# Prologue of a fused attention and FFN layer: FFN weight casts moved behind block 1's v, block 2's projections by seven products, last split of h behind a down product

## The chip, the cores and the metric

The kernel runs on one core of one Trainium2 chip, in one launch. The metric is device time in microseconds (us) from the first to the last instruction of that core; of several runs the median is told. Engines are named as in the profile: PE (TensorE, matrix products), PEld (its weight loads), DVE (VectorE), ACT (ScalarE), POOL (GpSimd), SP (SyncE, which only issues transfers here).

## The reference

There are 8192 tokens (4 x 2048) of 256 features. Everything is float32, and the FFN's weights arrive as int32.

```python
def _L0_attn_ref(x, W_q, W_k, W_v, W_g, W_o, log_decay):
    Q = x @ W_q.T; K = x @ W_k.T; V = x @ W_v.T
    mask = jnp.where(diff >= 0, decay ** diff, 0)          # within chunks of 32 tokens
    S = jnp.einsum('bncd,bnkd->bnck', Qc, Kc) * mask
    O = jnp.einsum('bnck,bnkd->bncd', S, Vc).reshape(B, T, D)
    gate = jax.nn.sigmoid(x @ W_g.T)
    return gate * O @ W_o.T + x

def _L0_ffn_ref(x, w_gate, w_up, w_down):                  # 256 -> 768 -> 256, int32 / 127
    h = jax.nn.silu(x @ wg.T) * (x @ wu.T)
    return h @ wd.T

x = _layernorm(x + _L0_attn_ref(x, ...))
x = _layernorm(x + _L0_ffn_ref(x, ...))
```

The queries and keys appear only in their product, so the kernel forms M = W_q.T @ W_k once and uses y = x @ M in place of both.

## The kernel before

**Tiling.** The tokens go in 16 blocks of 512 (`NB`, `TB`). A block passes these steps, each a function: `attn_gate` (sg, L460), `attn_y` (yT, L476), `attn_v` (v, L495), `attn_scores` (sT, L515), `attn_values` (goT, L536), `attn_out` (h: the product pa, L562, residual and layer norm), then h is turned so that features lie on partitions, the FFN's gate and up products in six chunks (`ffn_up`, fg and fu, L657), and the down product with the second layer norm (`ffn_down` fdn, L562, and `finish`).

**Three ways to do a projection or a turn.** For blocks 0 to 2, gate, y and v are plain products (eight quarter products each, with a 2 x 2 split of both operands). From block 3 on `split_gate`, `split_y`, `split_v` do them by seven quarter products (`seven`, L364 and L380): the operands' sums are made by POOL (`weight_sums` once for each weight, `token_sums` once for each block); four products fill four PSUM banks, three of them are copied out by ACT (L407), one sum is made by DVE (L409) and one by POOL (L411); then `others()` adds three more products onto the banks, and ACT, DVE (twice) and POOL write the four quarters. Block 0's and the last block's h are turned by PE (`transpose_h`, tile pt, with the high part hT_hi by ACT at L602 and the low part hT_lo by DVE at L603). All other blocks' h are turned by DVE and 16 small transfers (`move_h`, sq and hT, L617 and L623) and then split (`split_h`: hT_hi by ACT at L640, hT_lo by POOL at L641).

**High and low parts.** The FFN's products are done with a high and a low part of their operands. `integers` (L253) makes both parts of each weight by ACT casts from the int32 tiles, six casts for each of the three weights. Between the FFN's products, ACT takes s (L665), DVE forms u (L667, L669), ACT casts u_hi (L676) and POOL makes u_lo (L677).

**What orders the work.** A scheduler places the instructions of each engine; casts, splits and a few others are held in the order in which they are written. [...] PSUM has eight banks (`bank`), and each new one waits until the last reader of the bank it takes over is done. Two tokens-by-features buffers (`xin`, two of each kind) carry x, so block 2's xT can be loaded once block 0's scores are done.

**Stages.** A prologue does attention for blocks 0 and 1 and the projections of block 2. Then a loop (L746) takes for b = 0 to 13 the FFN of block b, the rest of block b+2's attention, and the projections of block b+3. An epilogue (from L790) does the FFN of blocks 14 and 15. In the prologue PE's order is: gate and v of block 0, M, gate of block 1, y of block 0, v of block 1, scores of 0, y of 1, values of 0, scores of 1, pa of 0, values of 1, then **y and v of block 2 (plain), pa of 1, gate of block 2 (plain), the turn pt of block 0**, and the first FFN product. ACT's order there is: v of 1, a table load, rstd of block 0 (L305), **12 casts of fg and fu, v of block 2, rstd of block 1, six casts of fd, a table load, gate of block 2 (L467), hT_hi of block 0**.

In the loop, `split_h` of block b+1 is written ahead of the last `ffn_up` chunk (L769). That holds for b = 13 too, where block 14's h is split. On ACT its two casts stand ahead of the last u_hi, on POOL its two subtractions stand ahead of the last u_lo:

```python
        ffn_up(b, hT, uT, range(4, 5))
        y_rest()
        hTs[b + 1] = split_h(b + 1, moving)
        ffn_up(b, hT, uT, range(5, KH))
```

Of the kernel before, what the change touches and what calls it, by code (L numbers as in the profile page):

```python
# [63 lines left out]
H_UP = 2.0**23  # L64
# [6 lines left out]
def kernel(  # L71
# [18 lines left out]
    KD = D // P  # L90
    KH = H // P
    NB = NT // TB

    const = ctx.enter_context(tc.tile_pool(name="const", bufs=1))
    setup = ctx.enter_context(tc.tile_pool(name="setup", bufs=2))
# [43 lines left out]
    wv = load_w(nc.scalar, w_vT, "wv")  # L139
    wq = load_w(nc.sync, w_q, "wq")  # L140
    wk = load_w(nc.scalar, w_k, "wk")
    if NB > 1:
        xTs[1] = load_xT(1)
    wo = load_w(nc.scalar, w_oT, "wo")
    xns[0] = load_xn(0)
    if NB > 1:
        xns[1] = load_xn(1)


    def pieces_of(t, i):  # L150
# [303 lines left out]
    def attn_gate(b):  # L454
        xt = xTs[b]
        sg = work.tile([P, KD, TB], F32, tag="sg", name=f"sg_{b}")
        for dc in range(KD):
            pg = bank(f"pg_{b}_{dc}")
            for ec in range(KD):
                nc.tensor.matmul(  # L460
                    pg,
                    lhsT=wg[:, ec, dc * P : (dc + 1) * P],
                    rhs=xt[:, ec, :],
                    start=(ec == 0),
                    stop=(ec == KD - 1),
                )
            nc.scalar.activation(sg[:, dc, :], pg, AF.Sigmoid)  # L467
        return sg

    def attn_y(b):  # L470
        xt = xTs[b]
        yT = work.tile([P, KD, TB], F32, tag="yT", name=f"yT_{b}")
        for fc in range(KD):
            py = bank(f"py_{b}_{fc}")
            for ec in range(KD):
                nc.tensor.matmul(  # L476
                    py,
                    lhsT=m_sb[:, ec, fc * P : (fc + 1) * P],
                    rhs=xt[:, ec, :],
                    start=(ec == 0),  # L480
                    stop=(ec == KD - 1),
                )
            nc.vector.tensor_copy(yT[:, fc, :], py)
        return yT

    def attn_v(b):
        xt = xTs[b]
        v = work.tile([P, NG, D], F32, tag="v", name=f"v_{b}")
        per = TB // D
        for h in range(NG // per):  # L490
            pv = bank(f"pv_{b}_{h}")
            for j in range(per):
                g = h * per + j
                for ec in range(KD):
# [201 lines left out]
    def finish(b, r, start=None):  # L696
        layer_norm(r, r, f"f{b}", on_r=H_UP)
        store(b, r, start)


    hs, hTs = {}, {}
    ys = {}
    first, second = 0, min(1, NB - 1)
    sg, v = attn_gate(first), attn_v(first)
    make_m()
    if second:
        sg_second = attn_gate(second)
    ys[first] = attn_y(first)
    if second:
        v_second = attn_v(second)  # L710
    sT = attn_scores(first, ys.pop(first))
    if second:
        ys[second] = attn_y(second)
    goT = attn_values(first, sT, v, sg)
    if second:
        sT_second = attn_scores(second, ys.pop(second))
    hs[first] = attn_out(first, goT, 1 if NB == 1 else H_UP)
    fg = integers(ffn_gT, ffn_int[0], "fg")
    fu = integers(ffn_uT, ffn_int[1], "fu")
    if second:  # L720
        goT = attn_values(second, sT_second, v_second, sg_second)
    x_sums = {}
    ahead = {}
    if NB > 2:
        xTs[2] = load_xT(2)
        ahead[2] = attn_y(2), attn_v(2)
    if second:
        hs[second] = attn_out(second, goT, 1 if NB == 2 else H_UP)
    fd = integers(ffn_dT, ffn_int[2], "fd")
    if NB > 2:  # L730
        ahead[2] += (attn_gate(2),)
    if NB > 3:
        for w, name in ((m_sb, "m"), (wg, "g"), (wv, "v")):
            w_sums[name] = weight_sums(w, name)
        xTs[3] = load_xT(3)
        x_sums[3] = token_sums(xTs[3], "x_3")
    hTs[first] = transpose_h(first, hs[first], 1 if NB == 1 else H_UP)


    half = range(KH // 2), range(KH // 2, KH)  # L740
    looked = 0

    def nothing():
        pass

    for b in range(NB - 2):  # L746
        n = b + 2
        m = n + 1 if n + 1 < NB else None
        xns[n] = load_xn(n)
        hT = hTs.pop(b)  # L750
        uT = [], []
        yT, v, sg = ahead.pop(n)
        ffn_up(b, hT, uT, range(0, 2))
        sT = attn_scores(n, yT)
        if m is not None and m + 1 < NB:
            xTs[m + 1] = load_xT(m + 1)
        moving = move_h(b + 1, hs[b + 1])
        ffn_up(b, hT, uT, range(2, 3))
        v_rest = y_rest = g_rest = nothing
        if m is not None:  # L760
            v_next, v_rest = split_v(m, x_sums[m])
        ffn_up(b, hT, uT, range(3, 4))
        v_rest()
        goT = attn_values(n, sT, v, sg)
        if m is not None:
            y_next, y_rest = split_y(m, x_sums[m])
        ffn_up(b, hT, uT, range(4, 5))
        y_rest()
        hTs[b + 1] = split_h(b + 1, moving)  # L769
        ffn_up(b, hT, uT, range(5, KH))  # L770
        if m is not None:
            sg_next, g_rest = split_gate(m, x_sums.pop(m))
        hs[n] = attn_out(n, goT, 1 if n == NB - 1 else H_UP)
        g_rest()
        if m is not None:
            ahead[m] = y_next, v_next, sg_next
            if m + 1 < NB:
                x_sums[m + 1] = token_sums(xTs[m + 1], f"x_{m + 1}")
        finish(b, ffn_down(b, uT, hs.pop(b)))
        if looked < top.shape[1]:  # L780
            look_up(looked)
            looked += 1
# [8 lines left out]
    per = NG // 2  # L791
    cols = [slice(i * per * P, (i + 1) * per * P) for i in range(2)]
    uT_last = [], []
    early = range(0)
    if NB > 1:
        uT = [], []
        ffn_up(last - 1, hTs[last - 1], uT, half[0])
        hTs[last] = transpose_h(last, hs[last], 1)
        ffn_up(last - 1, hTs[last - 1], uT, half[1])
        early = half[0]  # L800
        ffn_up(last, hTs[last], uT_last, early, cols[0])
        r_before = ffn_down(last - 1, uT, hs[last - 1])
        mv_before = moments(r_before, f"f{last - 1}")
    ffn_up(last, hTs[last], uT_last, range(len(early), KH), cols[0])
    ffn_up(last, hTs[last], uT_last, range(KH), cols[1])
    n_wide = count_wide()
# [28 lines left out]
            )  # L835
            in_turn(scaled)

    if NB > 1:
        std_before = root(mv_before, f"f{last - 1}", H_UP, order=in_turn)
    r = work.tile([P, NG, D], F32, tag="r2", name=f"r2_{last}")  # L840

    def store_group(g):
# [12 lines left out]
    for g in range(NG):  # L855
        pb = bank(f"fdn_{last}_{g}")[:, :D]
        terms = back_terms(g, uT_last, map(chunked, fd))
        for i, (part, w) in enumerate(terms):
            nc.tensor.matmul(
                pb,  # L860
                lhsT=part[:, g * P : (g + 1) * P],
                rhs=w,
                start=(i == 0),
                stop=(i == len(terms) - 1),
            )
        in_turn(
            nc.vector.scalar_tensor_tensor(
                r[:, g, :], pb, SCALE**3 / U_UP, hs[last][:, g, :], ALU.mult, ALU.add
            )
        )  # L870
        mv = moments(r, f"f{last}_{g}", [g], order=in_turn)
        if g == 0 and NB > 1:
            normalize(r_before, mv_before, std_before, f"f{last - 1}", H_UP)
            store(last - 1, r_before)
        std = root(mv, f"f{last}_{g}", groups=[g], order=in_turn)
        waiting.append((g, mv, std))
        if 0 < g < NG - 1:
            normalize_first()
        if g == NG - 2:
            normalize_first()  # L880
# [119 lines left out]
```

## Time and profile before

| what | value |
|---|---|
| time, median of 3 runs | 545.64 us (544.54 to 545.95) |
| span of the profiled execution | 545.3 us |
| prologue, up to the first FFN product | 56.89 us |
| one pass of the loop (91.58 to 123.60) | 32.02 us |
| ACT_TABLE_LOAD (L305 group) | 1283 ns each |
| HBM traffic | 53 GB/s over the span |

The profile's busy times are shares of the whole span, and the 14 passes of the loop weigh most in them. The change touches the prologue, the first pass and the last pass, so those stretches have to be read by themselves: the list of waits, the chain of work that ended last, and the stretches cut at the first FFN product and at the last down product of the loop. A row of the timeline or of the chain has the start, the length in us, the engine, the tile and the line; times are from the span's start. In the table by stretch, each engine has its busy time and in brackets how many instructions; after them come the granted clock of PE as a share of full speed, the share of the DMA engines, and GB/s.

### The profile page before, as it was taken

How to read it: one execution, taken by the hardware profiler on the slowest of the kernel's cores; microseconds unless marked ns; L12 is line 12 of the kernel's file. 1: busy time of each engine (PE TensorE's matmuls, PEld its weight loads, DVE VectorE, ACT ScalarE, POOL GpSimd, SP SyncE). 2: the span in 40 equal slices, each digit the busy share in tenths (PEclk: the TensorE clock that was granted, in tenths of full speed). 3: DMA queues.
4: the chain of work that ended last, by engine and by line, in shares of the span. 5: the costliest groups of instructions: out<-in, count | busy, mean ns of one | idle time of the engine just before them, and what ended most of it. 6: DMA issues, size and time to landing. Idle time of an engine off the chain costs nothing.

```text
span 545.3 us, 9852 instructions
## 1 busy us (share of the span) xinstructions
PE 527.8 (97%) x3462; PEld 419.8 (77%) x3462; DVE 387.7 (71%) x1019; ACT 306.9 (56%) x551; POOL 261.1 (48%) x295
## 2 busy tenths in 40 slices
PE   8998899999999999999999999999999999998992
PEld 5676588887878888787888878788887878876792
DVE  4266457769686776968777596867859686796873
ACT  2216455666466565646646574664657566464744
POOL 5120164563637456372645737265572726333552
PEclk9999799999999999999999999999999999999998
DMA  7531301413123141311314131141413112020102
GB/s 256 169 116 40 77 2 40 117 39 98 21 54 102 40 112 44 97 22 49 106 40 111 45 95 24 47 109 40 108 48 88 31 44 73 2 73 5 40 2 81
DMA packets 43126, 36.87 MB, mean 68 GB/s; under 512 B 4673, under 2 KB 38977, under 8 KB 43073
## 3 DMA queue, kind: packets, MB, share of 16 engines
q1 hardware_dynamic: 41952, 35.15, 22.7%
q10 hardware_dynamic: 1088, 1.05, 0.6%
q8 instruction: 29, 0.48, 0.4%
q14 instruction: 25, 0.20, 0.1%
q0 software_dynamic: 32, 0.00, 0.0%
HBM read 20.45 MB, written 8.39 MB: 53 GB/s over the span
## 4 chain that ended last, share of the span: by engine, by line
PE 90%; DVE 3%; ACT 2%; SPq 1%; POOL 1%; issue 1%; DMA 0%; DVEq 0%; ACTq 0%
PE fg L657 16%; PE fu L657 15%; PE fdn L562 14%; PE pa L562 10%; PE p_v L380 7%; PE p_y L364 7%; PE p_g L364 7%; PE po L536 5%; PE ps L515 3%; PE py L476 2%; PE pv L495 2%; PE pg L460 1%; SPq L623 1%; PE pi L178 1%; ACT L305 0%
## 5 line engine op out<-in xcount | busy, mean ns | idle before, releaser
L677 POOL TENSOR_TENSOR u_lo<-u,u_hi 128x512 f16<-128x512 f32 (+1 forms) x102 | 123.7, 1214 | 173.4 <-ACT u_hi L676 172.3
L667 DVE SCALAR_TENSOR_TENSOR s<-fg,s 128x512 f32<-128x512 f32 (+1 forms) x102 | 66.4, 651 | 51.8 <-ACT s L665 51.1
L665 ACT ACTIVATE s<-fg 128x512 f32<-128x512 f32 (+1 forms) x102 | 58.3, 571 | 74.6 <-PE fg L657 74.2
L657 PE MATMUL fg<-hT_hi,fg_hi 128*128 128x512 f32 (+1 forms) x204 | 74.7, 447 | 3.8 <-ACT hT_hi L602 3.8
L676 ACT CAST u_hi<-u 128x512 fp32r<-128x512 f32 (+1 forms) x102 | 60.4, 592 | 31.0 <-DVE u L669 30.1
L669 DVE TENSOR_TENSOR u<-fu,s 128x512 f32<-128x512 f32 (+1 forms) x102 | 66.1, 649 | 5.6 <-POOL u_lo L677 1.1
L657 PE MATMUL fu<-hT_hi,fu_hi 128*128 128x512 f32 (+1 forms) x204 | 62.0, 384 | 0.0
L657 PE MATMUL fg<-hT_lo,fg_lo 128*128 128x512 f16 (+1 forms) x204 | 59.8, 375 | 0.0
L657 PE MATMUL fu<-hT_lo,fu_lo 128*128 128x512 f16 (+1 forms) x204 | 59.0, 371 | 0.0
L562 PE MATMUL pa<-wo,goT 128*128 128x256 f32 x256 | 58.0, 379 | 0.0
L562 PE MATMUL fdn<-fd_hi,u_hi 128*128 128x256 f32 x360 | 55.7, 296 | 0.6 <-ACT u_hi L676 0.6
L562 PEld LDWEIGHTS pa<-wo,goT 128*128 128x128 f32 x256 | 48.6, 190 | 6.7
L641 POOL TENSOR_TENSOR hT_lo<-hT,hT_hi 128x512 f16<-128x512 f32 x28 | 35.3, 1282 | 27.6 <-ACT hT_hi L640 27.6
L562 PEld LDWEIGHTS fdn<-fd_hi,u_hi 128*128 128x128 f32 x360 | 46.8, 189 | 1.9 <-ACT u_hi L676 0.8
L562 PE MATMUL fdn<-fd_lo,u_lo 128*128 128x256 f16 x360 | 44.7, 274 | 1.8 <-POOL u_lo L677 1.8
L657 PEld LDWEIGHTS fg<-hT_hi,fg_hi 128*128 128x128 f32 x204 | 36.0, 191 | 12.9 <-ACT hT_hi L602 4.2
L657 PEld LDWEIGHTS fu<-hT_hi,fu_hi 128*128 128x128 f32 x204 | 37.7, 189 | 7.7
L305 ACT ACT_TABLE_LOAD x30 | 38.5, 1283 | 0.5
L562 PEld LDWEIGHTS <-u_lo 128*128 128x128 f16 x360 | 32.7, 98 | 6.9 <-POOL u_lo L677 2.1
L657 PEld LDWEIGHTS <-fu_lo 128*128 128x128 f16 x204 | 20.1, 99 | 22.2 <-DVE sT L525 1.2
L583 DVE SCALAR_TENSOR_TENSOR h<-x,pa 128x512 f32<-128x512 f32 x32 | 22.0, 688 | 20.6 <-PE pa L562 20.0
L657 PEld LDWEIGHTS <-fg_lo 128*128 128x128 f16 x204 | 16.0, 99 | 19.8 <-issue 13.3
(151 smaller groups left out, 980.4 us busy)
## 6 DMA issues: line engine op xcount, KB each, us to landing
x<-in_x_dram SPq DMA_DIRECT2D x16, 512.0 KB, 3.4
xT<-in_xT_dram SPq DMA_DIRECT2D x15, 512.0 KB, 4.4
out_dram<-r SPq DMA_DIRECT2D x15, 512.0 KB, 5.1
hT<-sq SPq DMA_DIRECT2D x224, 32.0 KB, 1.9
fg_int<-in_ffn_gT_dram SPq DMA_DIRECT2D x3, 256.0 KB, 8.3
fu_int<-in_ffn_uT_dram SPq DMA_DIRECT2D x3, 256.0 KB, 6.6
fd_int<-in_ffn_dT_dram SPq DMA_DIRECT2D x3, 256.0 KB, 6.0
xT<-in_xT_dram SPq DMA_DIRECT2D x2, 256.0 KB, 3.6
```

Of the source, the lines that this page charges most:

```text
L305: nc.scalar.activation(std[:, span], mv[:, span, 1], AF.Sqrt, bias=eps, scale=1 / on_r**2)
L364: nc.tensor.matmul(pb, lhsT=a[i - 1], rhs=b[i - 1], start=first, stop=True, skip_group_check=True,)
L380: nc.tensor.matmul(pb[:, g * P : (g + 1) * P], lhsT=b[i - 1][:, g * P : (g + 1) * P], rhs=a[i - 1], start=first and g == 0, stop=True, ski ...
L536: nc.tensor.matmul(po[:, cols], lhsT=v[:, g, dc * P : (dc + 1) * P], rhs=sT[:, cols], start=True, stop=True,)
L562: nc.tensor.matmul(pb[:, j * D : (j + 1) * D], lhsT=part[:, g * P : (g + 1) * P], rhs=w, start=(i == 0), stop=(i == len(terms) - 1),)
L641: nc.gpsimd.tensor_tensor(in_order[1], whole, in_order[0].bitcast(F32), ALU.subtract)
L657: nc.tensor.matmul(pb, lhsT=w[kind][:, dc, hc * P : (hc + 1) * P], rhs=hT[kind][:, dc, cols], start=(kind == kinds[0] and dc == 0), stop=( ...
L665: nc.scalar.activation(s, pg, AF.Sigmoid, scale=SCALE / H_UP)
L667: nc.vector.scalar_tensor_tensor(s, pg, U_UP / H_UP**2, s, ALU.mult, ALU.mult)
L669: nc.vector.tensor_tensor(u, pu, s, ALU.mult)
L676: nc.scalar.copy(hi, u)
L677: nc.gpsimd.tensor_tensor(lo, u, hi.bitcast(F32), ALU.subtract)
```

## The change

Three things are done. **The casts** of all three FFN weights are written right behind block 1's v, before block 0's scores, so that ACT does them while it has nothing else. **Block 2's v, y and gate** are no longer plain: they go through the seven-product forms, placed among the rest of the prologue. v's first four products come behind pa of block 0, its other three behind the values of block 1, y's first four ahead of pa of block 1, its rest behind the turn of block 0, the gate's first four ahead of the first FFN chunk and its rest behind that chunk. The weight sums then serve block 2 as well, and `token_sums` runs for block 2 in the prologue and for block 3 in the first pass. **In the last pass** (b = 13) `split_h` is written behind the down product. What else differs is the removal of branches for inputs of fewer than four blocks.

```diff
-ys[first] = attn_y(first)
-    v_second = attn_v(second)
-sT = attn_scores(first, ys.pop(first))
+yT = attn_y(0)
+v_1 = attn_v(1)
+fg = integers(ffn_gT, ffn_int[0], "fg")
+fu = integers(ffn_uT, ffn_int[1], "fu")
+fd = integers(ffn_dT, ffn_int[2], "fd")
+sT = attn_scores(0, yT)
+for w, name in ((wv, "v"), (m_sb, "m"), (wg, "g")):
+    w_sums[name] = weight_sums(w, name)
+xTs[2] = load_xT(2)
+x_sums = token_sums(xTs[2], "x_2")
...
-hs[first] = attn_out(first, goT, 1 if NB == 1 else H_UP)
-fg = integers(ffn_gT, ffn_int[0], "fg")
-fu = integers(ffn_uT, ffn_int[1], "fu")
-    goT = attn_values(second, sT_second, v_second, sg_second)
-    xTs[2] = load_xT(2)
-    ahead[2] = attn_y(2), attn_v(2)
-    hs[second] = attn_out(second, goT, 1 if NB == 2 else H_UP)
-fd = integers(ffn_dT, ffn_int[2], "fd")
-    ahead[2] += (attn_gate(2),)
-hTs[first] = transpose_h(first, hs[first], 1 if NB == 1 else H_UP)
+xTs[3] = load_xT(3)
+hs[0] = attn_out(0, goT)
+v, rest = split_v(2, x_sums)
+goT = attn_values(1, sT_1, v_1, sg_1)
+rest()
+yT, rest = split_y(2, x_sums)
+hs[1] = attn_out(1, goT)
+hTs[0] = transpose_h(0, hs[0])
+rest()
+sg, g_rest = split_gate(2, x_sums)
+ahead = yT, v, sg
...
-    ffn_up(b, hT, uT, range(0, 2))
+    ffn_up(b, hT, uT, range(0, 1))
+    if b == 0:
+        g_rest()
+        x_sums = token_sums(xTs[m], f"x_{m}")
+    ffn_up(b, hT, uT, range(1, 2))
...
-    hTs[b + 1] = split_h(b + 1, moving)
+    if more:
+        y_rest()
+        hTs[b + 1] = split_h(b + 1, moving)
     ffn_up(b, hT, uT, range(5, KH))
...
-    finish(b, ffn_down(b, uT, hs.pop(b)))
+    r = ffn_down(b, uT, hs.pop(b))
+    if not more:
+        hTs[b + 1] = split_h(b + 1, moving)
+    finish(b, r)
```

Built, the order on ACT in the prologue becomes: v of block 1, all 18 casts, three copies of v's products (L407), a table load, rstd of block 0, a quarter of v, three copies of y's products, hT_hi of block 0 (two), a quarter of y, rstd of block 1, three copies of the gate's products, a table load, s of the first FFN chunk, then the gate's quarters. In the last pass ACT's order becomes: last u_hi, table load, rstd of block 15, hT_hi of block 14; and POOL's: last u_lo, then hT_lo. The loop's other passes (b = 1 to 12) keep their order on every engine.

More of the change, by code (lines that the diff above doesn't have):

```diff
@@ L92 @@
     NB = NT // TB
+    assert NB > 3
     const = ctx.enter_context(tc.tile_pool(name="const", bufs=1))
@@ L141 @@
     wk = load_w(nc.scalar, w_k, "wk")
-    if NB > 1:
-        xTs[1] = load_xT(1)
+    xTs[1] = load_xT(1)
     wo = load_w(nc.scalar, w_oT, "wo")
     xns[0] = load_xn(0)
-    if NB > 1:
-        xns[1] = load_xn(1)
+    xns[1] = load_xn(1)
     def pieces_of(t, i):
@@ L701 @@
     hs, hTs = {}, {}
-    ys = {}
-    first, second = 0, min(1, NB - 1)
-    sg, v = attn_gate(first), attn_v(first)
+    sg, v = attn_gate(0), attn_v(0)
     make_m()
-    if second:
-        sg_second = attn_gate(second)
-    ys[first] = attn_y(first)
-    if second:
-        v_second = attn_v(second)
-    sT = attn_scores(first, ys.pop(first))
[L712 to L716, printed above, removed]
-    hs[first] = attn_out(first, goT, 1 if NB == 1 else H_UP)
+    sg_1 = attn_gate(1)
+    yT = attn_y(0)
+    v_1 = attn_v(1)
     fg = integers(ffn_gT, ffn_int[0], "fg")
     fu = integers(ffn_uT, ffn_int[1], "fu")
-    if second:
-        goT = attn_values(second, sT_second, v_second, sg_second)
-    x_sums = {}
-    ahead = {}
-    if NB > 2:
-        xTs[2] = load_xT(2)
-        ahead[2] = attn_y(2), attn_v(2)
-    if second:
-        hs[second] = attn_out(second, goT, 1 if NB == 2 else H_UP)
-    fd = integers(ffn_dT, ffn_int[2], "fd")
-    if NB > 2:
-        ahead[2] += (attn_gate(2),)
[L732 to L736, printed above, removed]
-    hTs[first] = transpose_h(first, hs[first], 1 if NB == 1 else H_UP)
+    fd = integers(ffn_dT, ffn_int[2], "fd")
+    sT = attn_scores(0, yT)
[3 more added lines that the diff above has]
+    x_sums = token_sums(xTs[2], "x_2")
+    yT = attn_y(1)
+    goT = attn_values(0, sT, v, sg)
+    sT_1 = attn_scores(1, yT)
+    xTs[3] = load_xT(3)
[9 more added lines that the diff above has]
+    ahead = yT, v, sg
     half = range(KH // 2), range(KH // 2, KH)
     looked = 0
-    def nothing():
-        pass
     for b in range(NB - 2):
         n = b + 2
-        m = n + 1 if n + 1 < NB else None
+        m = b + 3
+        more = m < NB
         xns[n] = load_xn(n)
@@ L751 @@
         uT = [], []
-        yT, v, sg = ahead.pop(n)
-        ffn_up(b, hT, uT, range(0, 2))
+        yT, v, sg = ahead
+        ffn_up(b, hT, uT, range(0, 1))
[3 more added lines that the diff above has]
+        ffn_up(b, hT, uT, range(1, 2))
         sT = attn_scores(n, yT)
-        if m is not None and m + 1 < NB:
+        if m + 1 < NB:
             xTs[m + 1] = load_xT(m + 1)
@@ L758 @@
         ffn_up(b, hT, uT, range(2, 3))
-        v_rest = y_rest = g_rest = nothing
-        if m is not None:
-            v_next, v_rest = split_v(m, x_sums[m])
+        if more:
+            v_next, v_rest = split_v(m, x_sums)
         ffn_up(b, hT, uT, range(3, 4))
-        v_rest()
+        if more:
+            v_rest()
         goT = attn_values(n, sT, v, sg)
-        if m is not None:
-            y_next, y_rest = split_y(m, x_sums[m])
+        if more:
+            y_next, y_rest = split_y(m, x_sums)
         ffn_up(b, hT, uT, range(4, 5))
-        y_rest()
-        hTs[b + 1] = split_h(b + 1, moving)
+        if more:
+            y_rest()
+            hTs[b + 1] = split_h(b + 1, moving)
         ffn_up(b, hT, uT, range(5, KH))
-        if m is not None:
-            sg_next, g_rest = split_gate(m, x_sums.pop(m))
+        if more:
+            sg_next, g_rest = split_gate(m, x_sums)
         hs[n] = attn_out(n, goT, 1 if n == NB - 1 else H_UP)
[L774 to L778, printed above, removed]
-        finish(b, ffn_down(b, uT, hs.pop(b)))
+        if more:
+            g_rest()
+            ahead = y_next, v_next, sg_next
+        if m + 1 < NB:
+            x_sums = token_sums(xTs[m + 1], f"x_{m + 1}")
+        r = ffn_down(b, uT, hs.pop(b))
+        if not more:
+            hTs[b + 1] = split_h(b + 1, moving)
+        finish(b, r)
         if looked < top.shape[1]:
@@ L793 @@
     uT_last = [], []
[L794 to L803, printed above, removed]
+    uT = [], []
+    ffn_up(last - 1, hTs[last - 1], uT, half[0])
+    hTs[last] = transpose_h(last, hs[last], 1)
+    ffn_up(last - 1, hTs[last - 1], uT, half[1])
+    early = half[0]
+    ffn_up(last, hTs[last], uT_last, early, cols[0])
+    r_before = ffn_down(last - 1, uT, hs[last - 1])
+    mv_before = moments(r_before, f"f{last - 1}")
     ffn_up(last, hTs[last], uT_last, range(len(early), KH), cols[0])
@@ L836, in normalize @@
             in_turn(scaled)
-    if NB > 1:
-        std_before = root(mv_before, f"f{last - 1}", H_UP, order=in_turn)
+    std_before = root(mv_before, f"f{last - 1}", H_UP, order=in_turn)
     r = work.tile([P, NG, D], F32, tag="r2", name=f"r2_{last}")
@@ L871 @@
         mv = moments(r, f"f{last}_{g}", [g], order=in_turn)
-        if g == 0 and NB > 1:
+        if g == 0:
             normalize(r_before, mv_before, std_before, f"f{last - 1}", H_UP)
```

## The prediction

> **What bounds it now.** I read the page's busy shares first, then PE's list of waits, then the chain of waits around the two waits that the list names, last the table by stretch.
>
> ```profile
> PE 527.8 (97%) x3462; PEld 419.8 (77%) x3462; DVE 387.7 (71%) x1019; ACT 306.9 (56%) x551; POOL 261.1 (48%) x295
> PEclk9999799999999999999999999999999999999998
> ```
>
> PE is the bound: 97% busy, the next engine 71%. The clock row has one slice with a 7, the fifth, which begins at 54.5 us. Time can be won by fewer products, by closing PE's gaps, or by keeping its clock up. The list of PE's waits (total, times, longest, in us):
>
> ```profile
> PE fg L657 <- ACT hT_hi L602: 3.8, 1, 3.8
> PE fdn L562 <- POOL u_lo L677: 1.8, 1, 1.8
> PE pi L178 <- DVE idle L175: 1.5, 1, 1.5
> PE fdn L562 <- ACT u_hi L676: 0.6, 1, 0.6
> ```
>
> Four waits in the whole span; the third is the start of the kernel. The chain of waits shows what is behind the first and, further down, behind the other two (start, length, engine, tile):
>
> ```profile
> 50.84 1.55 ACT fd_hi L253 x3
> 52.39 1.56 ACT fd_lo L253 x3
> 53.97 1.28 ACT L467
> 55.26 1.08 ACT sg L467 x2
> 56.89 1.28 PE fg L657 x2
> ...
> 490.46 1.89 DMA hT<-sq
> 492.57 0.63 ACT hT_hi L640
> 493.27 2.50 POOL hT_lo L641 x2
> 495.76 1.23 POOL u_lo L677
> 497.04 4.39 PE fdn L562 x37
> ```
>
> PE finished the turn pt at 53.09, but the hT_hi that it made possible stood in ACT's queue behind six casts of fd, a table load (the third row) and the gate. In the last pass, the split of h waited for its 16 transfers, and u_hi and u_lo, which were only queued behind it, came late. The table by stretch (PE, PEld, DVE, ACT, POOL busy; then granted clock, DMA share, GB/s):
>
> ```profile
> 52.05:56.89 4.84, 1.04 (x10) 0.80 (x8) 1.98 (x7) 4.81 (x9) 0.00 (x0) 0.85 0.14 37
> 56.89:63.28 6.39, 6.39 (x17) 3.10 (x17) 2.65 (x4) 1.40 (x3) 0.00 (x0) 0.58 0.24 51
> 63.28:91.58 28.30, 28.30 (x201) 24.04 (x201) 18.02 (x42) 15.68 (x30) 17.21 (x18) 1.00 0.15 43
> 489.45:501.27 11.82, 9.38 (x66) 8.18 (x64) 7.49 (x22) 5.47 (x8) 4.99 (x4) 1.00 0.05 11
> ```
>
> In the second row PE is "busy" all the time, but at a clock of 0.58: the long gap has an aftermath that no list of waits shows. After the shorter waits of the last row the clock stayed at 1.00.
>
> [...] the gap of 3.80 us was followed by 6.39 us at 0.58, those of 0.62 and 1.81 us by nothing. [...] Here POOL's four sums at 36.6 to 39.5 took 0.73 us each while DVE's goT beside them took 0.66, against 0.69 without them: no cost to price.
>
> **Part 1, the casts.** They take 1.55 us for three, so 18 take 9.3 us. In ACT's timeline the engine is done with block 1's v at 26.06 and then has a table load and an idle of 11.60 us ahead of rstd. The weights were issued by 15.83 and land 6 to 8 us later, so the casts run from 26.06 to 35.4. The first ACT work behind them, a copy of v's first product, cannot start before PE has finished that product at about 37.3. Cost nothing, hidden in ACT's idle time; the table load moves behind the copies.
>
> **Part 2, block 2 by seven.** Plain y, v and gate took 3.44, 3.45 and 3.43 us on PE's chain (38.44, 41.87, and 48.62 in the timeline). By seven, the first pass of the loop shows 1.78 + 1.34 for v and 1.73 + 1.29 for y and for the gate: 3.12, 3.02, 3.02. Saved: 10.32 - 9.16 = 1.16 us of PE. What is new is waits: each group's last three products wait for ACT's copies, and each new bank for its last reader. I lay PE's new order out from 36.65, where the chain has pa of block 0 end: v's four 1.78 to 38.43, values of block 1 1.78 to 40.21, v's three 1.34 to 41.55, y's four 1.73 to 43.28, pa of block 1 3.45 to 46.73, pt 0.87 to 47.60, y's three 1.29 to 48.89, gate's four 1.73 to 50.62, first FFN chunk. Then I ask of each wait when it is met:
>
> v's first needs xT of block 2, issued at 26.55, landing 3.4 to 4.4 us later, then POOL's sums, 4 x 0.7, by 34. v's three need the copies: in the first pass the third copy ends 1.91 us behind the first product, so 38.6 against 40.21. y's third and fourth banks need DVE's p6 sum (39.1) and goT (40.2), against 42.4 and 42.8. pa needs the second goT, behind rstd (the copies end at 38.6, load 1.28, rstd 0.30: 40.2), so 41.4 against 43.28. pt needs block 0's h (four times 0.34 behind it: 42.8) and the bank of v's last quarter (43.4), against 46.73. The gate's third bank needs block 1's second residual (46.73 + 0.2 + 0.7 = 47.7) against 49.75; its fourth a quarter of y from ACT, behind both hT_hi (48.9), against 50.2. The FFN's hT_hi is then ready at 48.5; hT_lo, whose DVE instruction also frees fg's bank, at 49.2 and 49.9, against 50.62 and 51.1. The thinnest margins are 1.2 to 1.4 us: nothing waits. Behind the gate's rest, 1.29 us to 53.7, the second chunk needs y's quarters from DVE (50.5 and 51.0). The new sums of block 3 can start only once the gate's rest has read the old ones, run 53.9 to 56.8 and are asked for at 58.9.
>
> What this is worth: the third FFN chunk began at 64.43 on the chain before. Now the first takes 1.80 us at full clock (the chain at 501.43 shows 0.46 + 0.46 + 0.45 + 0.43) to 52.42, the gate's rest is done at 53.71, the second chunk at 55.49, scores 1.08 at 56.57. **64.43 - 56.57 = 7.86 us.** Most of it is the gap of 3.80 us and the slow clock: two chunks took 6.39 us in place of 3.58, so 2.8. The rest, 1.26, is the saved products and rounding. I take 7.8.
>
> A transfer is put behind a new wait: SP now has the load of block 4's xT, which waits for block 2's scores, ahead of the last nine of the 16 transfers of block 1's h. Nine at 0.64 us from 56.8 and 1.9 us to land give 64.5; ACT reaches hT_hi in that pass at 77.43 - 7.8 = 69.6. Hidden.
>
> **Part 3, the last split.** From the start of pa to the first chunk of block 14 PE took 11.82 us (501.27 - 489.45). In the first pass the same work took 91.58 - 81.32 = 10.26, less 1.29 for the gate's rest that stands between: 8.97. So the two waits with their restarts cost 2.85 us, a little over their 2.43 of idle time. Without the split in front, u_hi follows u at 491.3 and ends at 492.0, u_lo at 493.3, asked for at about 493.3 and 494. The split itself now waits on ACT for rstd of block 15 (its sums end at 494.8): hT_hi 495.2 to 496.3, hT_lo 495.8 to 498.3. The first FFN chunk of block 14 now begins at 501.27 - 2.85 = 498.42 with the high part, the low part 0.9 later. Margin 1.0 for the second low half; nothing else is queued behind the split on POOL before then. **Gain 2.85 us.**
>
> Passes 1 to 12 keep their order, and PE has no wait in them. Sum: 545.64 - 7.8 - 2.85 = **535.0**.
>
> **Rivals.** (a) The gap closes, but a new wait of some 2 us takes its place ahead of the first FFN product (hT_lo or a PSUM bank late), or the clock falls all the same: 535.0 plus 2 to 2.8 gives 537.0 to 537.8. For it: many banks are handed over there, and margins are just over 1 us. Against: a wait under 2 us left the clock alone at 495, and every estimate above is from a row. (b) Only the tail works, the prologue trades its gap for three exposed copy chains: 545.64 - 2.85 - 1.16 = 541.6. Against: other PE work of 1.7 to 3.5 us lies between the halves of every group. (c) Slower: the gap at hT_hi stays, with its slow clock, and each of the three groups also exposes its 1.9 us of copies: 541.6 + 5.7 = 547.3. For it: ACT's and DVE's queues around the turn are full[...]. Against: the 11.60 us of idle time on ACT are there to take 9.3 us of casts. (d) Slightly better, 533.8, if banks and queues also fall better in the first pass; PE has no gap there, so little is left.
>
> **Chances.** Forecast 0.79, (a) 0.11, (b) 0.03, (c) 0.03, (d) 0.04. Of the forecast I allow 1.2 us either side for the medians and the layout; (a) reaches to 537.8, of which I take most: 533.7 to 537.4. The bound of 0.3% is 1.6 us, so faster is all of them but (c), less a little for what I have not thought of: 0.95; same 0.02; slower 0.03.
>
> **What would show it.** PE's list of waits should have only the start; the clock row no 7 in the fifth slice; ACT's casts in one row of 18 from 26.06; the first fg at about 50.6, the first loop pass's scores at about 55.5, and block 14's first fg about 10.7 us sooner than at 501.27. Wrong would be a wait of PE for hT_hi, hT_lo or for an ACT copy of over 1 us before the scores, or a wait for hT of block 14 behind the down product.

## The result and the profile after

The changed kernel takes **535.76 us** (median of 4 runs, 535.24 to 536.01), the kernel before 545.34 us in the same comparison (544.54 to 545.95). The ratio is 0.9824 with a 95% interval of 0.9807 to 0.9841: faster by 9.6 us. The forecast was 535.0, in a range of 533.7 to 537.4.

All line numbers of the new kernel are one lower than before (pa and fdn L561, fg and fu L656, casts L252, hT_hi of block 0 L601). PE's row of busy time and its clock row, from the page of the kernel after:

```profile
PE 522.8 (98%) x3486; PEld 421.0 (79%) x3486; DVE 391.2 (73%) x1026; ACT 310.8 (58%) x561; POOL 268.4 (50%) x305
PEclk9999999999999999999999999999999999999997
```

PE has 24 matrix products more in this count and is 5.0 us less busy. By the prediction's prices 1.2 us of that are saved products; most of the rest is the slow clock (0.58 over 6.39 us before), which counted as busy time: the 7 in the fifth slice is gone. The list of PE's waits of the kernel after (total, times, longest):

```profile
PE pi L177 <- DVE idle L174: 1.5, 1, 1.5
```

Only the start of the kernel is left; the waits for hT_hi, u_hi and u_lo are gone. The chain of the kernel after, around the place of the former gap (start, length, engine, tile, line, number of instructions):

```profile
46.05 0.87 PE pt L598 x8
46.92 1.30 PE p_y L363 x6
48.22 1.73 PE p_g L363 x8
49.95 0.46 PE fg L656 x2
...
51.76 1.29 PE p_g L363 x6
...
54.85 1.08 PE ps L514 x32
```

The chain stays on PE throughout. Behind the turn pt stand the rest of y and the gate's first four products, 3.03 us in all, and in that time hT_hi is made. ACT's timeline in the kernel after shows why hT_hi can be made so soon (start, length; in brackets the idle time before, and who ended it):

```profile
25.25 1.66 ACT L252 CAST fg_hi<-fg_int 128x512 fp32r<-128x512 int32 x3
...
33.04 1.66 ACT L252 CAST fd_lo<-fd_int 128x512 f16<-128x512 int32 x3
...
36.44 1.27 ACT L406 COPY p_v<-p_v 128x256 f32<-128x256 f32 x3 [1.74 <-PE p_v L379]
...
46.52 1.08 ACT L601 ACTIVATE hT_hi<-pt 128x512 fp32r<-128x512 f32 x2 [3.95 <-PE pt L598]
```

The casts end by 34.70, ACT then waits for PE's first product of v, and ahead of hT_hi it has been idle for 3.95 us: nothing stands in front of it in ACT's queue. In the last pass, the table by stretch from pa of block 15 to the first FFN product of block 14 (PE, PEld, DVE, ACT, POOL busy; clock, DMA share, GB/s):

```profile
480.95:489.92 8.97, 8.97 (x65) 8.20 (x64) 7.52 (x18) 5.57 (x8) 5.15 (x4) 1.00 0.09 18
```

The kernel before took 11.82 us for this, of which PE was busy 9.38. Now it is busy throughout.

The two profiled spans differ by 11.4 us, more than the 9.6 us of the medians, because the profiled execution of the kernel before was a long one: 547.08 us, where the median is 545.34.

### The profile page after: what moved, and what is told of

Same layout as the page of the kernel before. It is cut to its first block, busy times and chain, and to the rows that moved or that the text cites. A ratio compares the mean times of both kernels' runs of the same rounds, so it can differ in the third digit from the quotient of the medians.

```text
span 533.9 us, 9939 instructions
## 1 busy us (share of the span) xinstructions
PE 522.8 (98%) x3486; PEld 421.0 (79%) x3486; DVE 391.2 (73%) x1026; ACT 310.8 (58%) x561; POOL 268.4 (50%) x305
## 4 chain that ended last, share of the span: by engine, by line
PE 95%; DVE 2%; ACT 1%; issue 0%; DVEq 0%; POOL 0%
PE fg L656 16%; PE fdn L561 16%; PE fu L656 15%; PE pa L561 10%; PE p_v L379 8%; PE p_y L363 8%; PE p_g L363 8%; PE po L535 5%; PE ps L514 3%; PE pg L459 1%; PE py L475 1%; PE pv L494 1%; PE pi L177 1%; DVE u L668 1%; DVE s L666 1%
## 5 line engine op out<-in xcount | busy, mean ns | idle before, releaser
L656 PE MATMUL fg<-hT_hi,fg_hi 128*128 128x512 f32 (+1 forms) x204 | 74.0, 443 | 0.0
L656 PE MATMUL fu<-hT_hi,fu_hi 128*128 128x512 f32 (+1 forms) x204 | 61.6, 382 | 0.0
L656 PE MATMUL fg<-hT_lo,fg_lo 128*128 128x512 f16 (+1 forms) x204 | 58.9, 370 | 0.0
L656 PE MATMUL fu<-hT_lo,fu_lo 128*128 128x512 f16 (+1 forms) x204 | 58.1, 366 | 0.0
L561 PE MATMUL pa<-wo,goT 128*128 128x256 f32 x256 | 58.0, 379 | 0.0
L561 PE MATMUL fdn<-fd_hi,u_hi 128*128 128x256 f32 x360 | 55.4, 296 | 0.0
L561 PEld LDWEIGHTS pa<-wo,goT 128*128 128x128 f32 x256 | 48.6, 190 | 6.7
L561 PEld LDWEIGHTS fdn<-fd_hi,u_hi 128*128 128x128 f32 x360 | 46.8, 189 | 1.1
L561 PE MATMUL fdn<-fd_lo,u_lo 128*128 128x256 f16 x360 | 44.7, 274 | 0.0
L656 PEld LDWEIGHTS fu<-hT_hi,fu_hi 128*128 128x128 f32 x204 | 37.5, 188 | 7.7
L656 PEld LDWEIGHTS fg<-hT_hi,fg_hi 128*128 128x128 f32 x204 | 35.7, 189 | 8.5
L656 PEld LDWEIGHTS <-fu_lo 128*128 128x128 f16 x204 | 20.0, 98 | 21.5 <-DVE sT L524 1.2
L561 PEld LDWEIGHTS <-u_lo 128*128 128x128 f16 x360 | 32.7, 98 | 5.1 <-POOL u_lo L676 0.3
L535 PE MATMUL po<-sT,v 128*128 128x128 f32 x256 | 31.2, 275 | 0.0
```

Source lines behind the costliest of these rows:

```text
L535: nc.tensor.matmul(po[:, cols], lhsT=v[:, g, dc * P : (dc + 1) * P], rhs=sT[:, cols], start=True, stop=True,)
L561: nc.tensor.matmul(pb[:, j * D : (j + 1) * D], lhsT=part[:, g * P : (g + 1) * P], rhs=w, start=(i == 0), stop=(i == len(terms) - 1),)
L656: nc.tensor.matmul(pb, lhsT=w[kind][:, dc, hc * P : (hc + 1) * P], rhs=hT[kind][:, dc, cols], start=(kind == kinds[0] and dc == 0), stop=( ...
```

## The experiments

Two stretches hold everything that the change touches, and they are read from the timeline of each run. **A** runs from the start of block 0's scores (the first ps) to the start of block 2's scores (the third), **B** from pa of block 15 to the first FFN product of block 14. "A + B" is the sum of the two against the second profile of the kernel before (base_again); "measured" is the difference of the medians to the kernel before, run on the same chip.

| run | A, us | B, us | A + B against base_again | median, us | measured against before | ratio (95%) |
|---|---|---|---|---|---|---|
| before, profile of the prediction | 37.93 | 11.82 | +0.81 | 545.34 | | |
| base_again | 37.28 | 11.66 | 0 | 545.88 | +0.2 | 1.0005 (0.9995 to 1.0016) |
| casts_only | 32.26 | 11.72 | -4.96 | 541.28 | -4.4 | 0.9917 (0.9899 to 0.9934) |
| tail_only | 37.27 | 8.98 | -2.69 | 543.09 | -2.6 | 0.9952 (0.9938 to 0.9966) |
| casts_tail | 32.25 | 8.97 | -7.72 | 538.01 | -8.1 | 0.9845 (0.9828 to 0.9862) |
| filler | 35.36 | 13.58 | 0 | 545.44 | -0.2 | 0.9997 (0.9987 to 1.0007) |
| filler6 | 36.42 | 11.70 | -0.82 | 546.42 | +0.8 | 1.0005 (0.9993 to 1.0016) |
| filler_tail | 35.37 | 8.97 | -4.60 | 540.95 | -5.1 | 0.9905 (0.9890 to 0.9921) |
| turn_early | 31.27 | 13.13 | -4.54 | 540.26 | -4.9 | 0.9908 (0.9887 to 0.9929) |
| turn_tail | 31.27 | 8.97 | -8.70 | 537.08 | -8.0 | 0.9852 (0.9831 to 0.9874) |
| old_tail | 30.11 | 12.19 | -6.64 | 538.89 | -7.2 | 0.9879 (0.9854 to 0.9903) |
| casts_late | 30.40 | 8.97 | -9.57 | 535.94 | -9.7 | 0.9820 (0.9807 to 0.9833) |
| after_again | 30.11 | 8.97 | -9.86 | 535.70 | -10.4 | 0.9802 (0.9786 to 0.9819) |
| after | 30.12 | 8.97 | -9.85 | 535.76 | -9.6 | 0.9824 (0.9807 to 0.9841) |

The two stretches account for every median within 0.7 us but that of filler6, which is taken up below. So the answer to where the time came from lies in A and B. Block 2's products by sevens have no run in which they alone are changed; their share is a difference between runs.

### base_again: the kernel before, profiled a second time

No edit.

> The kernel before, unchanged, profiled once more. The two profiles differ by 11.4 us (545.3 and 533.9), the medians by 9.6. Theory V (PE's slow clock varies from run to run): the stretch behind the 3.80 us gap was 6.39 us long at a clock of 0.58 in the profile before, but is shorter in most executions; then this profile's span is 543 to 544.5, its first loop scores begin at 61.5 to 62.8 (63.35 in the profile before), counted from an equal start, or its first 8 us are shorter by 0.7. Rival F (the profile before is typical and the changed kernel loses 1.8 us elsewhere in its timed runs): span 545.3 again, with the same 6.39 us behind the gap, and a timed median that is the span plus 1.75 us, about 547.

Median 545.88 us. The waits are nearly the same (3.8, 1.8 and 0.5 us), but the two FFN chunks behind the long one are shorter. The table by stretch of base_again, from the first fg to block 2's scores, cut as in the prediction's second row:

```profile
56.69:62.43 5.74, 5.74 (x16) 2.65 (x17) 2.65 (x4) 1.40 (x3) 0.00 (x0) 0.70 0.24 50
```

The mean clock was 0.70 here against 0.58 in the profile of the prediction, and the stretch took 5.74 us against 6.39. The length of the slow clock differs from execution to execution; tail_only has 5.73 (56.47 to 62.20 in its timeline). What sets it was not shown.

### casts_only: only the casts moved

```diff
     v_second = attn_v(second)
+    fg = integers(ffn_gT, ffn_int[0], "fg")
+    fu = integers(ffn_uT, ffn_int[1], "fu")
+    fd = integers(ffn_dT, ffn_int[2], "fd")
...
-fg = integers(ffn_gT, ffn_int[0], "fg")
-fu = integers(ffn_uT, ffn_int[1], "fu")
...
-fd = integers(ffn_dT, ffn_int[2], "fd")
```

> Only the casts moved behind block 1's v; block 2's y, v and gate plain, split of h in the last pass as before. If the casts alone are what the gap is made of: the wait for hT_hi shrinks from 3.80 us to what is left of a table load, the gate's two sigmoids and hT_hi behind the plain gate's end at about 52.0 (gate 52.2 to 53.3, hT_hi to 54.4 against pt's end at 53.1, so 1.0 to 1.5 us), the clock stays up behind it, and the time falls by 2.5 us for the gap and by 1 to 2.8 us for the clock: 540 to 542. If the seven products are needed for the gap to close (rival), the gap stays over 3 us and the time falls by less than 1.5 us.

Median 541.28 us. PE's list of waits in casts_only:

```profile
PE fg L657 <- ACT hT_hi L602: 0.7, 1, 0.7
```

ACT's timeline in casts_only shows what is left in front of hT_hi:

```profile
50.86 1.28 ACT L467 ACT_TABLE_LOAD   x1
52.15 1.09 ACT L467 ACTIVATE sg<-pg 128x512 f32<-128x512 f32 x2
53.12 1.10 ACT L602 ACTIVATE hT_hi<-pt 128x512 fp32r<-128x512 f32 x2
```

Without the casts, the table load and the gate still stand ahead of hT_hi. The wait shrinks from 3.8 to 0.7 us, and after 0.7 us the clock stays up (3.83 us from the first fg to the next scores, 5.74 in base_again): A is 5.02 us shorter, 3.12 of it the wait (3.81 to 0.69 in the timeline) and 1.90 behind it, where the clock was slow before.

### tail_only: only the last split moved

```diff
-        hTs[b + 1] = split_h(b + 1, moving)
+        if m is not None:
+            hTs[b + 1] = split_h(b + 1, moving)
...
+        r = ffn_down(b, uT, hs.pop(b))
+        if m is None:
+            hTs[b + 1] = split_h(b + 1, moving)
```

> Only the last pass's split of h behind the down product; prologue as before. Forecast's part 3: 2.85 us less than the kernel before, pa to block 14's first fg in 8.97 us in place of 11.82, no wait of PE for u_hi or u_lo: ratio 0.9948. Rival (the split's wait moves to block 14's first fg, or to the last turn): at most 1 us gained, with a wait of fg for hT_hi or hT_lo in PE's list.

Median 543.09 us. B falls from 11.66 to 8.98, 2.68 us, and A is unchanged. The median says the same, 2.6 us.

### casts_tail: both, with block 2 left plain

The edits of casts_only and of tail_only together.

> Casts behind block 1's v and the last split of h behind the down product, but block 2's v, y and gate plain. If the parts add: 545.6 less 4.4 (casts alone) less 2.6 (tail alone) = 538.6, and the seven products are then worth what is left to the changed kernel's 535.8, some 2.8 us: 1.2 us of products, 0.7 us of the wait for hT_hi that stays with the casts alone, and its restart. If theory T holds, it is 0.5 to 2 us lower than that sum (536.5 to 538), because the casts' kernel pays for a drop of the clock at the tail, which this one cannot.

Median 538.01 us; A is that of casts_only, B that of tail_only. The two parts add up. What is left to after_again, on the same chip, is 2.3 us: by the profiles 2.14 in A, 0.7 of it the last wait for hT_hi.

### filler and filler_tail: the slow clock without the gap's time

Four products on zeros stand behind the turn pt, so that PE works where it would wait. They end before hT_hi comes, and take no time of their own.

```diff
 hTs[first] = transpose_h(first, hs[first], 1 if NB == 1 else H_UP)
+filler = bank("filler")
+for _ in range(4):
+    filled = nc.tensor.matmul(
+        filler, lhsT=idle[:, :P], rhs=idle, start=True, stop=True
+    )
+    tc.keep_in_program_order(filled)
```

> The kernel before with four products on the zeroed tile idle written between the turn pt and the first FFN chunk; nothing reads them. PE has the same work held back by hT_hi, but is not idle. If the long gap costs a second time through the clock: the stretch from the first fg to the first scores falls from 6.39 to 3.6 us in the profile, granted clock 1.00 in it, and the time falls by that clock's cost alone, 1 to 2.8 us. Rival (the slow clock there has nothing to do with idle time, or four products on zeros do not keep the clock): 6.39 us and 0.58 again, time the same.

filler gains nothing: 545.44 us. The table by stretch of filler, its first row from the first fg to block 2's scores, the second in the last pass:

```profile
56.26:60.08 3.82, 3.82 (x17) 2.05 (x17) 2.22 (x4) 1.40 (x3) 0.00 (x0) 1.00 0.24 51
494.00:499.00 5.00, 4.97 (x31) 4.55 (x32) 2.35 (x7) 0.14 (x1) 0.00 (x0) 0.66 0.00 0
```

In the prologue the clock is at 1.00 and A is 1.92 us shorter. But in the last pass, where the waits for u_hi and u_lo still are, the clock now falls (0.66 is its mean over the 5 us shown), and B is 1.92 us longer: 0.36 of it a longer wait for u_hi (0.82 us against 0.46 in base_again), the rest behind the wait for u_lo. The timeline of PE in filler, behind that wait:

```profile
494.03 1.30 PE L562 MATMUL fdn<-fd_lo,u_lo 128*128 128x256 f16 x7 [1.80 <-POOL u_lo L677]
494.99 2.91 PE L562 MATMUL fdn<-fd_hi,u_hi 128*128 128x256 f32 x12
```

In the kernel before, these seven and twelve products took 0.94 and 1.67 us:

```profile
497.04 0.94 PE L562 MATMUL fdn<-fd_lo,u_lo 128*128 128x256 f16 x7 [1.81 <-POOL u_lo L677]
497.73 1.67 PE L562 MATMUL fdn<-fd_hi,u_hi 128*128 128x256 f32 x12
```

To see whether the filler is worth its 1.9 us where those two waits are gone, filler_tail has the edit of filler and that of tail_only.

> Four products on zeros in the gap behind the turn, and the last pass's split of h behind the down product. The filler alone kept the clock up in its profile behind the turn (3.89 us from the first fg to the scores, 5.81 in the second profile before), but its profile lost about the same at the down product of the last pass, where the waits of 0.8 and 1.8 us were followed by half-speed products. Theory T (the two tail waits drop the clock in most executions of the filler kernel, and cost the filler's gain again): with the tail waits gone the filler shows its worth, 1.5 to 2.2 us below the tail edit alone, 541.0 to 541.6, ratio 0.991 to 0.992. Rival N (in timed executions the clock behind the turn costs next to nothing, the profile's 1.9 us is an exception): no better than the tail edit alone, 542.7 to 543.3, ratio 0.995 to 0.996.

Median 540.95 us. B is 8.97, A 35.37, and the ratios of filler_tail and tail_only, 0.9905 and 0.9952, lie 0.0047 apart, 2.6 us; by the medians it is 2.1 us, by the profiles 1.9. So **the slow clock behind the 3.8 us gap costs some 2 us**, and in the filler kernel what was won there was lost again 430 us later.

### filler6: six products in place of four

```diff
-for _ in range(4):
+for _ in range(6):
```

> Six products on zeros in the gap behind the turn in place of four; last pass as in the kernel before. PE is then busy 1.72 us longer there, 0.37 us of which fill the wait that four left, so all behind it comes 1.35 us later. With four, the tail waits dropped the clock in most executions and cost some 1.95 us. Theory W [...]: with the tail moved by 1.35 us [...] the clock stays up in most executions, and the longer kernel is no slower: 544.6 to 545.8, ratio 0.998 to 1.000, granted clock 0.994 to 0.995 in most executions. Rival (any two waits of this size drop the clock once nothing dropped it before): 546.4 to 547.2, ratio 1.002 to 1.003, clock 0.991 to 0.992.

Median 546.42 us, at the edge of the rival's range; the ratio, 1.0005, is in neither theory's. The two additional products shift everything behind them (the wait for hT_hi is gone, A is 1.06 us longer than with four), to see if the place of the last pass's waits in time decides on the clock. In the profiled execution it did not fall (1.00 over 494.63 to 498.87), and B is 11.70. But of 22 executions, 11 had a mean clock of 0.992 or less and took 546.4 to 548.1 us, while the ten at 0.994 or more took 544.0 to 545.5. With four products 17 of 22 had 0.992 or less. The mean of an execution doesn't tell where the clock fell, and only one of the 22 has a profile, so whether the place of the waits decides was not shown.

### after_again and old_tail: the changed kernel, and with the split in its old place

```diff
         if more:
             y_rest()
-            hTs[b + 1] = split_h(b + 1, moving)
+        hTs[b + 1] = split_h(b + 1, moving)
...
-        if not more:
-            hTs[b + 1] = split_h(b + 1, moving)
```

> The changed kernel, unchanged, timed in the same job as the kernels that take parts of it away. Time 535.2 to 536.4; profile 533.3 to 534.6, PE's only wait the start. The difference to the kernel before should again be 9.6 us and not the forecast's 10.65; a profile span of 533.9 with a span of 544.5 before (second profile) makes 10.6.

> The changed kernel with only the split of h put back ahead of the last FFN chunk in the last pass. Forecast's part 3: 2.85 us slower than the changed kernel, 538.6, with PE's waits of 0.6 and 1.8 us back. Theory T: those waits drop the clock here in many executions, as nothing dropped it before: 3.5 to 4.8 us slower, 539.3 to 540.6, and a profile with half-speed fdn behind them. Rival N: 2.4 to 3.0 us slower.

after_again has 535.70 us, and its A and B are those of after to 0.01 us. It is 10.4 us faster than the kernel before in its comparison, not the 9.6 that were expected; the kernel before had 546.06 us there. The 9.85 us of the profiles lie between the two. old_tail has 538.89, 3.2 us more, and B is 12.19 against 8.97: 3.22 us. The split's place is thus worth 3.2 us beside the other two parts and 2.7 alone; the difference is the wait for u_hi, 1.00 us here and 0.46 in base_again. In the profile of old_tail the clock stayed up (1.00 over 484 to 499) behind waits of 1.0 and 1.8 us; one of its six executions had a mean clock of 0.987 and took 542.24.

### casts_late: the casts put back, all else changed

```diff
-fg = integers(ffn_gT, ffn_int[0], "fg")
-fu = integers(ffn_uT, ffn_int[1], "fu")
-fd = integers(ffn_dT, ffn_int[2], "fd")
...
 hs[0] = attn_out(0, goT)
+fg = integers(ffn_gT, ffn_int[0], "fg")
+fu = integers(ffn_uT, ffn_int[1], "fu")
...
 hs[1] = attn_out(1, goT)
+fd = integers(ffn_dT, ffn_int[2], "fd")
```

> The changed kernel with the casts put back: 12 casts of fg and fu behind pa of block 0, six of fd behind pa of block 1; seven products and the last split as in the change. Tests whether block 2's seven products need the casts out of ACT's way. By rows: rstd of block 0 ends at 39.3 of the changed profile, 12 casts run to 45.5, so the quarter of v that frees a bank for the second half of pa ends at 46 in place of 40.5, against 44.3 when PE asks for it: a wait of 1.6 us; then hT_hi behind y's copies, and the gate's copies behind fd's casts, some 4 us late: a further wait of 1 to 3 us around the gate's rest. Theory: 538.3 to 541 with two or more new waits of PE for ACT. Rival (banks and spare work absorb it; the casts matter only for hT_hi): within 1 us of the changed kernel, 535.3 to 536.7.

Median 535.94 us, the same as the changed kernel. The theory that the gap stays closed only with the early casts falls here: not one of its new waits came. ACT's timeline in casts_late:

```profile
39.52 1.64 ACT L252 CAST fg_hi<-fg_int 128x512 fp32r<-128x512 int32 x3
...
46.82 1.09 ACT L601 ACTIVATE hT_hi<-pt 128x512 fp32r<-128x512 f32 x2
...
49.20 1.65 ACT L252 CAST fd_hi<-fd_int 128x512 fp32r<-128x512 int32 x3
```

The 12 casts run beside PE's work up to pa of block 1, and fd's six stand behind hT_hi, because in the changed kernel pt comes right behind pa of block 1 and hT_hi goes ahead of rstd of block 1. PE waits nowhere but at the start. A is 0.28 us longer, all of it behind the first fg; there the scheduler also placed the gate's rest inside the second chunk, which was no part of the edit.

### turn_early and turn_tail: only the order of the turn

If the order is the cure, it should work in the kernel before, with nothing else changed: the turn of block 0 is written ahead of fd's casts and block 2's gate.

```diff
     hs[second] = attn_out(second, goT, 1 if NB == 2 else H_UP)
+    hTs[first] = transpose_h(first, hs[first], 1 if NB == 1 else H_UP)
 fd = integers(ffn_dT, ffn_int[2], "fd")
     ahead[2] += (attn_gate(2),)
-hTs[first] = transpose_h(first, hs[first], 1 if NB == 1 else H_UP)
```

> The kernel before with one edit: the turn of block 0's h (pt, hT_hi, hT_lo) is written ahead of fd's casts and of block 2's gate; casts at their old places, block 2 plain, last pass as before. Since the changed kernel with late casts was as fast as the changed kernel, the casts' place seems not to be what closes the gap. Theory Q (what counts is what stands ahead of hT_hi in ACT's queue, and behind pt in PE's): hT_hi follows v of block 2 at once, PE has the plain gate's 3.43 us to do meanwhile, the wait for hT_hi goes from 3.80 to 0, the clock stays up: 5.3 to 6.3 us faster than before, 539.3 to 540.3, which is more than the casts alone brought (4.4). Rival (the gap moves: fd's casts, the table load and the gate's sigmoids now hold back the first s and with it PSUM banks): a new wait of 2 us or more in the first chunks, 541.3 or slower.

Median 540.26 us. PE's list of waits in turn_early:

```profile
PE fdn L562 <- POOL u_lo L677: 1.8, 1, 1.8
PE pi L178 <- DVE idle L175: 1.5, 1, 1.5
PE fdn L562 <- ACT u_hi L676: 0.3, 1, 0.3
```

The wait for hT_hi is gone altogether: with pt ahead of the plain gate, its 3.44 us of PE work cover hT_hi. A is 6.01 us shorter, more than with the casts moved. But here, too, the clock fell at the waits of the last pass (its mean was 0.68 over 488.60 to 494.00). The timeline of PE in turn_early, in the last pass:

```profile
489.00 1.33 PE L562 MATMUL fdn<-fd_lo,u_lo 128*128 128x256 f16 x7 [1.82 <-POOL u_lo L677]
489.98 2.91 PE L562 MATMUL fdn<-fd_hi,u_hi 128*128 128x256 f32 x12
```

It took B to 13.13. Three of the six executions had a mean clock of 0.992 like this one (540.5 to 541.6 us), three had 0.994 or 0.995 (539.5 to 540.0). With the tail's edit added (turn_early and tail_only together):

> As turn_early, and the last split of h behind the down product. What is left to the changed kernel is then block 2 by seven products and the casts' place alone. Theory Q: 536.6 to 537.3, with PE's list of waits as short as in the changed kernel, and the changed kernel is faster only by the saved products, 1.2 us (0.5 to 1.6 measured). Rival as for turn_early: 538.5 or slower.

Median 537.08 us; B is 8.97, and PE waits only at the start. **One moved line and the tail's edit bring 8.0 of the 9.6 us.** What after has over turn_tail is A, 31.27 against 30.12: 1.15 us, against 1.16 forecast for the products that block 2 saves by the seven. The comparison also moves the casts; casts_late, with the casts late as in turn_tail, has 0.87 us, and the other 0.28 are those behind its first fg.

## Why the prediction was right

**Part 1, the casts at no cost.** Right: they stand in one row from 25.25 to 34.70 (forecast from 26.06, but the first scores began 0.69 us earlier in this execution), and ACT waits for PE behind them.

**Part 2, the layout.** Right, nearly to the number. From block 0's scores on, with the 0.69 us taken off, the first FFN product was forecast 50.62 - 0.69 = 49.93 and came at 49.95; the third chunk 56.57 - 0.69 = 55.88 and came at 55.93. None of the banks or copies asked for was late. The thinnest margin was the one named: DVE's second hT_lo ended at 48.89 in the timeline, 1.1 us ahead of the first fg. The saved 1.16 us measured 0.87 to 1.15 (casts_late and after against turn_tail).

**Part 3, the tail.** The forecast of 8.97 us for the stretch was met exactly. ACT and POOL finished the split at 487.8 and 490.0, ahead of its use.

**The term that was mis-sized** is "two chunks took 6.39 us in place of 3.58, so 2.8". The 6.39 came from one execution, and the length of the slow clock varies: base_again and tail_only show 5.74 and 5.73, which makes 2.2 in place of the 2.8. A fell by 7.16 us from base_again and not by the forecast's 7.8; the difference is this term. The tail's 2.85 measured 2.69 (B), also because it was read from one execution: the wait for u_hi was 0.62 us in that profile and 0.46 in base_again. The sum, 9.85 in place of 10.65, is the measured 9.6 within 0.3 us.

**What the prediction did not separate.** It names what stood ahead of hT_hi in ACT's queue (six casts, a table load, the gate) and prices the closed gap as one thing. The change has two cures for it, either of which closes most: moving the casts alone leaves a wait of 0.7 us (casts_only), moving the turn alone leaves none (turn_early), and with the turn in its new place the casts' place is worth nothing that the medians can tell (casts_late). So the 9.3 us of casts that part 1 places with care were not needed for the gain.

**The readings behind it.** That 3.80 us were followed by a slow clock and 0.62 and 1.81 us by nothing is true of that profile, but two waits of about that size were followed by a slow clock in filler (0.82 and 1.80 us) and turn_early (0.34 and 1.82 us): the length of a wait alone does not tell. "No cost to price" for POOL beside DVE was read from goT alone. The changed kernel shows a cost elsewhere: the 64 scalings of h (L319) take 0.41 us each with POOL idle, but one took 0.83 us beside POOL's sum of the gate, and one 1.37 us beside hT_lo of the moved split. Neither made PE wait.

**The rivals.** (a) was a new wait or a fallen clock, for 537.0 to 537.8: neither came. Its counter-argument, "a wait under 2 us left the clock alone at 495", held in the profile of before but is not general: behind the wait for u_lo, filler and turn_early took 5.80 us to block 14's first FFN product where base_again took 4.23. The argument did no harm, because the change removes these waits; that it came out right was luck. (b), only the tail works, would have shown as a wait in A; there is none. (c), slower, needed copy chains exposed in each group, and PE's chain shows none of them: its pieces follow each other without a break. (d), 533.8, needed gaps in the first pass, where before had none.

## What to carry to other kernels

Where PE waits for a result of another engine, read the queue of that engine in front of it: writing the wanted work earlier is as good as moving the work that stands in its way, and two such cures of one gap don't add.

A gap of PE can also cost what the clock loses behind it, here 1.9 to 2.6 us behind one of 3.8. Take that from several executions, since it varied by 0.65 us here for the same gap. Do not take short waits for harmless from one profile: here two waits of under 2 us were followed by a slow clock in two profiles and not in five others. And count a closed gap only when the other waits of the kernel are closed too, because the slow clock turned up behind them in filler: 5.80 us behind the wait for u_lo, where base_again took 4.23.

## What the runs showed of the hardware

**PE's clock fell behind two short waits in some profiles and not in others.** For each profile that has both waits of the last pass, in us: the two waits, the seven and the twelve down products behind the second, and the mean clock over a stretch behind or around it:

| profile | wait for u_hi | wait for u_lo | 7 products | 12 products | clock (stretch) |
|---|---|---|---|---|---|
| turn_early | 0.34 | 1.82 | 1.33 | 2.91 | 0.68 (488.60 to 494.00) |
| filler | 0.82 | 1.80 | 1.30 | 2.91 | 0.66 (494.00 to 499.00) |
| base_again | 0.46 | 1.82 | 0.94 | 1.67 | 1.00 (494.00 to 505.00) |
| filler6 | 0.50 | 1.81 | 0.94 | 1.67 | 1.00 (494.63 to 498.87) |
| casts_only | 0.52 | 1.81 | 0.94 | 1.67 | 1.00 (482.00 to 494.00) |
| before | 0.62 | 1.81 | 0.94 | 1.67 | 1.00 (489.45 to 501.27) |
| old_tail | 1.00 | 1.81 | 0.94 | 1.67 | 1.00 (484.00 to 499.00) |

The length of the waits does not order them: together they are shortest in turn_early, 2.16 us, where the clock fell, and longest in old_tail, 2.81 us, where it stayed up. What decides was not shown.

**The cost of the slow clock.** Behind the 3.8 us gap, the stretch from the first fg to the next scores took 6.39 us at a mean clock of 0.58 in the profile of the prediction, 5.74 at 0.70 in base_again, 5.73 in tail_only, and 3.82 at 1.00 in filler, where the gap is filled. That is 2.6 and 1.9 us more than filler's. In the profile of the prediction the clock was at 0.50 from 55.41 to 62.24, of which 5.35 us lie behind the start of the first fg. At half speed half of them are lost, 2.7 us by estimate, close to the 2.6 measured.

**ACT took its queue in order.** In the last pass of before, DVE had the last u ready at 491.33, but ACT stood idle for 2.16 us, until the transfers of hT had landed, did hT_hi from 492.57 on, and came to u_hi only at 493.62. In after, where hT_hi stands behind it, u_hi began 0.09 us behind its u (482.83 and 482.92).
